# A transformer block on 16 images: LN2 without centring and with its scale transposed as a column, a fourth product in 96 jobs, ten bands of 30 convolved by TensorE, and a new order

## Chip, core and metric

The kernel runs on one core of a Trainium2 chip. The metric is device time of one launch in microseconds; the figure for the kernel before is the median of three runs.

## The reference

The input x is 16 images of 128 channels and 96 x 96 pixels in float32. With channels last, per image:

```python
xn1 = layernorm(x, ln1_w, ln1_b)              # over the 128 channels, for each pixel
q, k, v = xn1 @ wq.T, xn1 @ wk.T, xn1 @ wv.T  # 8 heads of 16 channels
q, k = l2norm(q), l2norm(k)                   # each channel over all 9216 pixels
attn = softmax(einsum('hcn,hdn->hcd', q, k) / 4)       # channels against channels
x = x + (attn @ v) @ wp.T
xn2 = layernorm(x, ln2_w, ln2_b)              # (x - mean) / sqrt(var + eps), then w and b
h1 = w_in @ xn2                               # 128 -> 512 channels
h2 = depthwise 3x3 convolution of h1, zero padding of one pixel
x = x + w_out @ gelu(h2)                      # 512 -> 128 channels
```

## The kernel before, in words

Channels lie on the 128 partitions, pixels along the free dimension. An image is 8 bands of 12 rows (1152 pixels), a band three units of 4 rows (384 pixels). The work of all 16 images is one stream: while the bands of an image go through the feed-forward part, the first norm of the next image is done beside them.

*Norms (`norm`).* Tiles of 512 pixels are brought to pixels-on-partitions by TensorE into one of four PSUM banks named h (`forth`). For LN1 (names with _a) this is a transpose of x (L662). For LN2 (_b) it is a product with the matrix `centre`, which subtracts the mean over channels as well (L658). ScalarE copies the tile to a buffer zT in SBUF (L694), VectorE takes its statistics with two bn_stats, of two 128-pixel groups each (L669, tile st), and GpSimd makes the variance (L674), raises it to the power -1/2 (L678, rstd) and multiplies zT by rstd (L700). For LN1 the scaled zT is also multiplied with itself into the Gram matrix (L707), from which `attention` makes one 128 x 128 matrix per image. TensorE then transposes zT back (`channels`, `back`, L745), and ScalarE places the result in the ring buffer xn of rows with a column of padding (L751; for LN2 with a bias, L749).

*Second x (`x2`).* TensorE applies the image's matrix to LN1's xn (`mix`, L610), ScalarE writes that into an x tile (L619), and GpSimd's DMA adds the input x onto it (L622).

*Feed-forward (`conv_job`, `by_matmuls`, `ffn_out`).* The 512 hidden channels are four chunks. A job is one chunk of one band. TensorE makes its hidden rows (L932) and ScalarE copies them into a padded buffer h1 (L937; two halo rows, L928). The nine taps of the convolution are divided by the centre tap, so that the centre costs no multiplication. Three of the eight others are products made by ScalarE (L948, tiles pr): one is added to h1 by GpSimd (L951, tile merged), one onto the other by an accumulating DMA (L973), and that sum onto the result by a second accumulating DMA (L976). VectorE does five as multiply-adds: the first reads h1 and merged (L960), the middle ones go on in the PSUM tile acc (L964), the last writes the result h3 (L960). ScalarE applies gelu (L980). In 41 bands the fourth chunk is no job: TensorE convolves it with nine matrices `comp` that combine input projection and tap (L1041), and gelu reads PSUM (L1051). Last, four products over the chunks (L1069), VectorE's addition onto x (L1076) and the store.

*The order.* Nothing in the stream is ordered by a loop. Each piece of work is registered with its engine, an estimate of its duration, a place (a turn plus a constant from the table `AT`, and a rank), and the buffers that it reads and writes. `Plan.order` then runs a list scheduler with buffer pools over all of them: an idle engine takes the ready piece of the lowest place, a result counts as there after its duration plus a margin (`SLACK`, `T_LAND` for DMAs). The order of starts becomes the program order of each engine, and the engines wait for one another by semaphores:

```python
def pe(ns, p, f, r, w):
    op("PE", ns, p, f, r, w, ns + 200 + SLACK, ns)
def dve(ns, p, f, r, w, two=False, own=120):
    op("DVE", ns, p, f, r, w, ns + 120 + SLACK, ns + own, two=two)
def add(p, f, r, w):
    op("POOL", 890, p, f, r, w, T_LAND + SLACK, dma=T_ADD)
```

An op marked `two` (a VectorE op with two SBUF operands, a GpSimd op on whole tiles) is kept by the plan from running beside another such op.

Of the kernel before, what the change touches and what calls it, by code (L numbers as in the profile page):

```python
# [9 lines left out]
F32 = mybir.dt.float32  # L10
# [13 lines left out]
TINY = 1e-20  # L24
# [8 lines left out]
FOURTHS = ()  # L33
# [3 lines left out]
QT = 4  # L37
# [7 lines left out]
PR_BUFS = 7  # L45
H3_BUFS = 8
ZT_BUFS = 7
IN_TURN = ("zT", "tr", "h3", "pr", "xb", "x1")
AT = dict(
    load_w=-15.9, weights=1106.95, zeros=-4389.1, load_a=-21.95, forth_a=-14.05, stats_a=1086.6,  # L50
    variance_a=-3642.25, power_a=-2095.25, pool_product=152.05, merge=-3089.75, scaled_a=-3192.7, gram=420.15,
    back_a=-250, place_a=-142.6, attention=-21.5, mix=810.75, residual=204, mixed=-263.1, add_x=-3629.7,
    forth_b=-10.3, stats_b=962.7, variance_b=-3011.35, power_b=-3726.4, shift_b=20.9, scaled_b=-4386.5,
    back_b=285.25, place_b=-290.45, halo=-471.5, hidden=418.3, kept=-390.75, products=-596.2, add_last=-2869,
    tap=3.65, add_first=-4251.35, gelu=-9.7, conv=421.7, conv_gelu=4.3, out=422.65, add=865.75, store=-21.95,
    mix_0=421.5, residual_0=864.15, mixed_0=-612, add_x_0=-4213.25, gram_0=419.75, forth_a_0=-276.85,
    forth_b_0=-13.8, stats_a_0=1145.4, stats_b_0=866.4, scaled_a_0=-4479.8, copied_a=-299.2, copied_b=-393.1,
    copied_a_0=-390.45, copied_b_0=-1293.75, scaled_b_0=-3010.5, back_a_0=420.4, back_b_0=262, place_a_0=-286.8,
    place_b_0=11.4, shift_b_0=22.8, late=384.05,
)  # L60
# [12 lines left out]
T_ADD, T_MOVE, T_LAND = 2950, 1400, 500  # L73
# [11 lines left out]
class Plan:  # L85
# [7 lines left out]
    def __init__(self, **pools):  # L93
        self.free = {p: list(range(n)) for p, n in pools.items()}
        self.slot = {}
        self.ops, self.writer, self.readers, self.users = [], {}, {}, {}
        self.dma = 0.0
        self.two = self.held = self.lost = 0.0
# [31 lines left out]
    def order(self):  # L130
# [38 lines left out]
        def dispatch(engine, time):  # L169
# [22 lines left out]
            elif engine == "POOL":  # L192
                rest = max(0, self.two - time)
                ns, result, own = rest + ns, rest + result, rest + own
                if o[9]:
                    self.held = time + ns
            if o[9] and engine == "DVE":
                rest = max(0, self.held - time)
                ns, result, own = rest + ns, rest + result, rest + own
# [44 lines left out]
def tile_restormer_block(  # L244
# [81 lines left out]
    per_unit = const.tile([P, NCH], F32, name="per_unit")  # L326
    nc.scalar.dma_start(out=dw, in_=w_dw.rearrange("(n p) o kh kw -> p n (o kh kw)", p=P))
# [17 lines left out]
    small = ctx.enter_context(tc.tile_pool(name="small", bufs=4))  # L345
# [43 lines left out]
    def x_unit(of, i, u):  # L389
# [5 lines left out]
        tr=TR_BANKS, bk=BK_BANKS, h=H_BANKS, g=1, batch=4, zT=ZT_BUFS, x1=X1_BUFS, xb=XB_BUFS, pr=PR_BUFS, h3=H3_BUFS  # L395
# [44 lines left out]

    def zeros(p):


        def around(t, r):
            nc.gpsimd.memset(t[:, : r * WP].rearrange("p (r w) -> p r w", w=WP)[:, :, :1], 0.0)
            nc.gpsimd.memset(t[:, r * WP :], 0.0)
# [3 lines left out]
        for t in h1s:  # L450
            op("POOL", 1000, at("zeros", p), lambda t=t: around(t, BR + 2), [], [("w", "in")], 1200)

    def weights(p):
# [66 lines left out]
        def shifts():  # L520

            nc.vector.tensor_tensor(none, w2, w2, ALU.mult)
            nc.vector.tensor_scalar(none, none, TINY * TINY, TINY, ALU.is_lt, ALU.mult)
            nc.vector.tensor_add(w2, w2, none)
# [629 lines left out]
```

## Time and profile before

| | us |
|---|---|
| median of three runs (lowest, highest) | 4097.78 (4095.37, 4105.1) |
| profiled execution, its own time | 4102.59 |
| its span | 4100.9 |
| TensorE (PE) busy | 3936.4 |
| VectorE (DVE) busy | 3904.0 |
| ScalarE (ACT) busy | 3718.0 |
| GpSimd (POOL) busy | 3456.0 |

The page comes from one execution. Busy time is the time in which an engine runs at least one instruction; a matmul in float32 shows as two passes (two instructions), a transpose as one. Matmul ends are modelled, so PE may show busy where it is not at its peak. PEld is TensorE's weight load. A row of the groups reads: line, engine, operation, output<-inputs, shapes, count | busy us, mean ns of one | idle us of the engine before them, and what ended it. A row of the waits reads: who <- for whom: us in total, times, longest.

### The profile page before, as it was taken

Reading aid. Unit: us, or ns where it says so; the run is one execution under the profiler, and the core shown is the slowest. Engines: PE = TensorE matmul, PEld = TensorE weight load, DVE = VectorE, ACT = ScalarE, POOL = GpSimd, SP = SyncE. Lnnn points to the kernel's source line nnn. Section 1 sums busy time; section 2 is a strip of 40 time slices with the busy share of each in tenths; the row PEclk is TensorE's granted clock in tenths of the full one; section 3 lists DMA queues with packets and bytes.
Section 4 is the critical chain, followed back from the end, with each engine's and each line's share of the span. In section 5 each row is a group of like instructions: output and inputs, shape, how many; then the busy total and the mean of one; then the engine's idle time right before and its main releaser. Section 6 shows DMA issues by size and latency. Waiting matters only on the chain.

```text
span 4100.9 us, 52028 instructions
## 1 busy us (share of the span) xinstructions
PE 3936.4 (96%) x17409; PEld 2593.9 (63%) x17409; DVE 3904.0 (95%) x4170; ACT 3718.0 (91%) x5675; POOL 3456.0 (84%) x3320
## 2 busy tenths in 40 slices
PE   8999999999999999999999999999999999999999
PEld 6666666666666666666666566666666666566555
DVE  6999999999999999999999999999999999999998
ACT  4999999999999989899999999989999999899985
POOL 5988888797898979889788888978989889788774
PEclk9999999999999999999999999999999999999999
DMA  2999999998999999999999999989999999988996
GB/s 84 192 190 198 192 194 191 191 211 180 205 194 200 199 186 211 185 194 197 187 203 193 196 190 201 212 183 200 193 200 213 188 202 192 199 185 180 198 182 139
DMA packets 192846, 782.20 MB, mean 191 GB/s; under 512 B 22337, under 2 KB 23745, under 8 KB 192577
## 3 DMA queue, kind: packets, MB, share of 16 engines
q0 software_dynamic: 153072, 627.05, 80.4%
q1 hardware_dynamic: 38256, 151.73, 10.4%
q8 instruction: 137, 2.24, 0.2%
q14 instruction: 133, 1.08, 0.1%
q10 hardware_dynamic: 1248, 0.09, 0.0%
HBM read 148.85 MB, written 75.50 MB: 55 GB/s over the span
## 4 chain that ended last, share of the span: by engine, by line
PE 31%; DVE 20%; DMA 11%; ACT 11%; POOL 9%; issue 5%; POOLq 0%; DVEq 0%; SPq 0%; ACTq 0%
PE h L1069 9%; DVE acc L964 9%; PE h L932 7%; DMA h<-pr 6%; PE h L1041 5%; ACT pr L948 4%; DVE acc L960 4%; DVE h L960 3%; POOL merged L951 3%; DMA x<-in_x_dram 3%; PE h L658 2%; PE h L610 2%; PE h L745 2%; DMA pr<-pr 2%; POOL zT L700 2%
## 5 line engine op out<-in xcount | busy, mean ns | idle before, releaser
L964 DVE SCALAR_TENSOR_TENSOR acc<-h,ratio,acc 128x1140 f32<-128x1140 f32 (+2 forms) x1416 | 1949.4, 1377 | 18.2
L948 ACT ACTIVATE pr<-h,ratio 128x1152 f32<-128x1152 f32 x1410 | 1782.5, 1289 | 45.2 <-DMA pr<-pr 27.3
L951 POOL TENSOR_TENSOR merged<-pr,h 128x1152 f32<-128x1152 f32 x470 | 1249.5, 2659 | 72.8 <-DVE acc L960 44.8
L1069 PE MATMUL h<-h,woutT 128*128 128x384 f32 x3072 | 1122.3, 489 | 11.7 <-DVE x L1076 7.1
L932 PE MATMUL h<-xn,winT 128*128 128x384 f32 (+2 forms) x2826 | 1086.4, 495 | 24.2 <-DVE x L1076 9.0
L1041 PE MATMUL h<-xn,comp 128*128 128x380 f32 (+2 forms) x2214 | 794.1, 483 | 2.8 <-ACT h L937 2.3
L1069 PEld LDWEIGHTS h<-h,woutT 128*128 128x128 f32 x3072 | 560.0, 191 | 350.1 <-issue 14.8
L960 DVE SCALAR_TENSOR_TENSOR acc<-h,ratio,merged 128x1152 f32<-128x1152 f32 x470 | 753.2, 1602 | 26.8 <-POOL merged L951 11.6
L932 PEld LDWEIGHTS h<-xn,winT 128*128 128x128 f32 x2826 | 506.3, 190 | 357.8 <-issue 36.6
L937 ACT COPY h<-h 128x384 f32<-128x384 f32 (+2 forms) x1413 | 670.8, 511 | 63.4 <-PE h L932 58.4
L976 POOL DMA_DIRECT2D h<-pr x470 | 496.0, 1056 | 253.3 <-PE h L1069 39.3
L960 DVE SCALAR_TENSOR_TENSOR h<-h,ratio,acc 128x1152 f32<-128x1152 f32 x471 | 662.0, 1406 | 7.6 <-PE h L1069 1.2
L980 ACT ACTIVATE h<-h 128x1152 f32<-128x1152 f32 (+1 forms) x473 | 561.4, 1187 | 101.7 <-DMA h<-pr 94.6
L973 POOL DMA_DIRECT2D pr<-pr x470 | 492.9, 1055 | 136.9 <-ACT pr L948 100.5
L1041 PEld LDWEIGHTS h<-xn,comp 128*128 128x128 f32 x2214 | 398.9, 190 | 229.3 <-ACT h L937 6.8
L745 PEld LDWEIGHTS h<-ident,zT 128*128 128x128 f32 x2232 | 273.5, 141 | 240.9 <-issue 81.3
L678 POOL TENSOR_TENSOR rstd_a<-ve_a,mhalf 128x4 f32<-128x4 f32 x288 | 416.4, 1521 | 1.0
L745 PE MATMUL h<-ident,zT 128*128 128x128 f32 x2232 | 357.5, 276 | 49.8 <-POOL zT L700 31.8
L700 POOL TENSOR_TENSOR zT<-zT,rstd_a 128x512 f32<-128x512 f32 x270 | 384.9, 1451 | 1.9
L678 POOL TENSOR_TENSOR rstd_b<-ve_b,mhalf 128x4 f32<-128x4 f32 x288 | 362.1, 1258 | 9.9
L700 POOL TENSOR_TENSOR zT<-zT,rstd_b 128x512 f32<-128x512 f32 (+1 forms) x288 | 357.7, 1243 | 5.2
L694 ACT COPY zT<-h 128x512 f32<-128x512 f32 x553 | 318.4, 613 | 38.2 <-PE h L658 28.0
(178 smaller groups left out, 4263.4 us busy)
## 6 DMA issues: line engine op xcount, KB each, us to landing
pr<-pr POOLq DMA_DIRECT2D x470, 576.0 KB, 7.0
h<-pr POOLq DMA_DIRECT2D x470, 576.0 KB, 7.3
x<-in_x_dram SPq DMA_DIRECT2D x128, 576.0 KB, 6.7
out_dram<-x SPq DMA_DIRECT2D x127, 576.0 KB, 5.4
x<-in_x_dram POOLq DMA_DIRECT2D x123, 576.0 KB, 7.5
out_dram<-x SPq DMA_DIRECT2D x3, 192.0 KB, 1.9
h<-in_L_conv_w_in_dram SPq DMA_DIRECT2D x1, 256.0 KB, 3.0
h<-in_L_conv_w_out_dram SPq DMA_DIRECT2D x1, 256.0 KB, 3.1
```

Source lines behind the costliest of these rows:

```text
L678: nc.gpsimd.tensor_tensor(rstd, d["ve"], mhalf, ALU.pow)
L700: engine.tensor_tensor(z, z, rstd.unsqueeze(2).to_broadcast([P, len(ks), P]), ALU.mult)
L745: nc.tensor.transpose(d["pB"][:, j * P : (j + 1) * P], zTs[q][:, k, :P], ident)
L932: nc.tensor.matmul(rows(ph), lhsT=winT[:, n, :], rhs=window(xn, r0 + r, e - r, 1), start=True, stop=True)
L937: nc.scalar.copy(window(h1_, r, e - r, 1), rows(d.pop(("ph", r))))
L948: nc.scalar.activation(to, shifted(t), AF.Copy, scale=ratio[:, n, t : t + 1])
L951: nc.gpsimd.tensor_tensor(merged, d["pr", dma_taps[0]], shifted(UNIT), ALU.add)
L960: nc.vector.scalar_tensor_tensor(to, shifted(t), ratio[:, n, t : t + 1], also, ALU.mult, ALU.add)
L964: nc.vector.scalar_tensor_tensor(to, shifted(t)[:, lo:hi, cut], ratio[:, n, t : t + 1], to, ALU.mult, ALU.add)
L980: nc.scalar.activation(h3, h3, AF.Gelu)
L1041: nc.tensor.matmul(d["pc"][:, lo:hi, cut], lhsT=comp[:, t, :], rhs=window(xn, r0 + dy, UR, dx)[:, lo:hi, cut], start=(t == order[0]), stop ...
L1069: nc.tensor.matmul(rows(d["po"]), lhsT=woutT[:, n, :], rhs=h3s[g, n][:, s * UR : (s + 1) * UR, :], start=(k == 0), stop=(k == NCH - 1),)
```

## The change

LN2's tiles are now plain transposes, they are not copied out of PSUM (the statistics read PSUM), and zT is not scaled or transposed back. Instead rstd, a column per 128 pixels, is broadcast along the free dimension and transposed by TensorE, which gives each channel's partition the scale of each pixel; VectorE multiplies x by it into xn. The centring is folded into the weights at the start (`centre` applied to `winT` and `comp`). LN2's bias is folded as well: h1's padding holds a constant in place of zero, each gelu adds a bias column `ksum` (another one for an image's first and last row, so there gelu is split), and the convolution by TensorE gets one more small product for the two edge columns (`edgeT`). As h1's padding now takes part, VectorE's taps run over the full width.

```diff
-PE_BANDS = (0, 3, 6, 10, 13, 16, 20, 23, 26)
+PE_BANDS = (0, 3, 6, 9, 12, 15, 18, 21, 24, 27)
-FOURTHS = ()
+FOURTHS = ((0, 1, (0,)),)
-PR_BUFS = 7
+PR_BUFS = 8
-ZT_BUFS = 7
+ZT_BUFS = 4
+BATCHES = 8
 AT = dict(
-    load_w=-15.9, weights=1106.95, zeros=-4389.1, load_a=-21.95, forth_a=-14.05, stats_a=1086.6,
+    load_w=-10696.6, weights=-1325.7, zeros=-1188.75, load_a=-32.75, forth_a=537.05, stats_a=22,
...
-RANK = dict(tap=-69.4, products=649.2, forth_a=-922.65, forth_b=-118.15, conv_gelu=-62.7, mix=-456.4)
+RANK = dict(tap=-712.55, products=1729.15, forth_a=-347.95, forth_b=-713.5, conv_gelu=-713.7, mix=-53.4)
+LATE = 400
-T_ADD, T_MOVE, T_LAND = 2950, 1400, 500
+T_ADD, T_MOVE = 2950, 1400
+T_LAND = 1000
...
             elif engine == "POOL":
-                rest = max(0, self.two - time)
+                rest = max(0, self.two - time) if k != self.ahead else 0
...
             if o[9] and engine == "DVE":
                 rest = max(0, self.held - time)
+                head = queues["POOL"][0][1] if queues["POOL"] and not idle["POOL"] else None
+                if head is not None and ops[head][9] and room(head) is None:
+                    rest, self.ahead = max(rest, self.pool_free + ops[head][1] - time), head
...
-    def inside(t, r0, n):
+    def inside(t, r0, n, padded=False):
-        cut = slice(max(0, 1 - dx), W - max(0, dx - 1))
+        cut = slice(0, W) if padded else slice(max(0, 1 - dx), W - max(0, dx - 1))
...
+        def centred_in():
+            pc = v["pc3"] = bank(("weights", "centred in"))
+            nc.tensor.matmul(pc, lhsT=centre, rhs=winT.rearrange("p n c -> p (n c)"), start=True, stop=True)
...
                 for k in range(QT):
-                    if second:
-                        nc.tensor.matmul(
-                            d["pT", q][:, k, :], lhsT=xt[:, j * P : (j + 1) * P], rhs=centre, start=True, stop=True
-                        )
-                    else:
-                        nc.tensor.transpose(d["pT", q][:, k, :], xt[:, j * P : (j + 1) * P], ident)
+                    nc.tensor.transpose(d["pT", q][:, k, :], xt[:, j * P : (j + 1) * P], ident)
...
-                nc.vector.bn_stats(d["st"][:, j, :], zT(qs[h])[:, k : k + 2, :P].rearrange("p t c -> p c t"))
+                of = d["pT", qs[h]] if second or DIRECT else zT(qs[h])[:, :, :P]
+                nc.vector.bn_stats(d["st"][:, j, :], of[:, k : k + 2, :].rearrange("p t c -> p c t"))
...
-            for h, q in enumerate(qs):
+            for h, q in enumerate(qs if not second else ()):
...
-                    nc.tensor.transpose(d["pB"][:, j * P : (j + 1) * P], zTs[q][:, k, :P], ident)
+                    if second:
+                        of = rstds[q // QB][:, q % QB * QT + k : q % QB * QT + k + 1].to_broadcast([P, P])
+                    else:
+                        of = zTs[q][:, k, :P]
+                    nc.tensor.transpose(d["pB"][:, j * P : (j + 1) * P], of, ident)
 
             def place():
                 if second:
-                    nc.scalar.activation(interior(i, u), rows(d["pB"]), AF.Identity, bias=b2)
+                    nc.vector.tensor_tensor(interior(i, u), rows(x_unit(xbs, i, u)), rows(d["pB"]), ALU.mult)
...
         def step(engine, ns, also=(), reads=(), writes=mine):
-                op(engine, ns, s, f, [("w", "qk"), *reads], [*writes, *also], ns + 200 + SLACK)
+                op(engine, ns, s, f, [("w", "qk"), *reads], [*writes, *also], ns + 200 + LATE)
...
         def gelu(s0, s1):
-            h3 = h3_of(g, n)[:, s0 * UR : s1 * UR, :]
-            nc.scalar.activation(h3, h3, AF.Gelu)
+            for r0, r1, z in row_parts(b, s0 * UR, s1 * UR):
+                h3 = h3_of(g, n)[:, r0:r1, :]
+                nc.scalar.activation(h3, h3, AF.Gelu, bias=ksum[:, z, n : n + 1])
...
+            if t == order[-1]:
+                for k0, k1, z in parts:
+                    nc.tensor.matmul(
+                        d["pc"][:, k0 - s * UR : k1 - s * UR, 0 : W : W - 1], lhsT=edgeT,
+                        rhs=ident[:6, 2 * z : 2 * z + 2].unsqueeze(1).to_broadcast([6, k1 - k0, 2]),
+                        start=False, stop=(k0, k1, z) == parts[-1],
+                    )
...
+    zeros(-17.0)
     weights(-17.0)
-    zeros(-17.0)
```

With `FOURTHS`, the jobs of the first chunk in an image's six inner bands (96 jobs) have four products; the fourth is added to merged by GpSimd in an op of its own (L1030 after; the code for it stood in the kernel before, unused).

What the new order does is seen on three engines at the same place of the program, LN2 of image 4. TensorE first: the three tiles of 512 pixels that hold the end of band 2 and most of band 3 (x2_4_2, x2_4_3) go into banks h_1 to h_3. Before:

```order
L658 MATMUL h_1_74<-centre_83,x2_4_2_7442 128x128 x3
L658 MATMUL h_1_74<-centre_83,x2_4_3_7550 128x128
L662 MATMUL h_2_75<-ident_78,x_5_4_7333 128x128 x4
L658 MATMUL h_3_76<-centre_83,x2_4_3_7550 128x128 x4
L1069 MATMUL h_0_73<-h3_2_151,woutT_119 128x384
L1069 MATMUL h_0_73<-h3_7_156,woutT_119 128x384
L745 MATMUL h_1_74<-ident_78,zT_4_161 128x128
L745 MATMUL h_1_74<-ident_78,zT_2_159 128x128 x2
```

After:

```order
L708 MATMUL h_1_74<-ident_78,x2_4_2_7383 128x128 x3
L708 MATMUL h_1_74<-ident_78,x2_4_3_7549 128x128
L708 MATMUL h_2_75<-ident_78,x2_4_3_7549 128x128 x4
L708 MATMUL h_3_76<-ident_78,x2_4_3_7549 128x128 x4
L1120 MATMUL h_0_73<-xn_128,comp_124 128x384
L1120 MATMUL h_0_73<-xn_128,comp_124 128x4x95
L1120 MATMUL h_0_73<-xn_128,comp_124 128x384
L1120 MATMUL h_0_73<-xn_128,comp_124 128x4x95 x2
L661 MATMUL h_1_74<-xn_128,mwT_4_7099 128x384
```

The three LN2 tiles now stand one behind the other in three of the four banks, the fourth bank takes a convolution by TensorE, and the mix (L661) is the next to use bank h_1. On VectorE the same tiles' statistics (st_b4_6 to st_b4_8) stood so before:

```order
L669 BN_STATS st_b4_6_7685<-zT_6_163 128x6
L960 SCALAR_TENSOR_TENSOR acc_77<-h1_0_137,ratio_106,merged_141 128x1152
L669 BN_STATS st_b4_6_7685<-zT_6_163 128x6
L964 SCALAR_TENSOR_TENSOR acc_77<-h1_0_137,ratio_106,acc_77 128x12x95
L1076 TENSOR_TENSOR x2_3_7_6750<-h_0_73,x2_3_7_6750 128x384
L964 SCALAR_TENSOR_TENSOR acc_77<-h1_0_137,ratio_106,acc_77 128x12x95
L669 BN_STATS st_b4_7_7729<-zT_1_158 128x6
```

and after, from between the first tile's two on:

```order
L1036 SCALAR_TENSOR_TENSOR acc_77<-h1_0_141,ratio_106,merged_145 128x1152
L716 BN_STATS st_b4_6_7717<-h_1_74 128x6
L1040 SCALAR_TENSOR_TENSOR acc_77<-h1_0_141,ratio_106,acc_77 128x1152
L716 BN_STATS st_b4_7_7735<-h_2_75 128x6
L1040 SCALAR_TENSOR_TENSOR acc_77<-h1_0_141,ratio_106,acc_77 128x1152
L716 BN_STATS st_b4_7_7735<-h_2_75 128x6
L1036 SCALAR_TENSOR_TENSOR h3_6_160<-h1_0_141,ratio_106,acc_77 128x1152
L716 BN_STATS st_b4_8_7758<-h_3_76 128x6
L1036 SCALAR_TENSOR_TENSOR acc_77<-h1_1_142,ratio_106,merged_145 128x1152
L716 BN_STATS st_b4_8_7758<-h_3_76 128x6
L1040 SCALAR_TENSOR_TENSOR acc_77<-h1_1_142,ratio_106,acc_77 128x1152
L812 TENSOR_TENSOR xn_128<-x2_4_2_7383,h_1_74 128x4x96
```

The statistics now read the banks themselves, each second one a tap behind the first, and the placing (L812, xn from x and a bank) has come to VectorE. On GpSimd the same tile's small ops before:

```order
L674 TENSOR_SCALAR ve_b4_6_7727<-st_b4_6_7685 128x4
L678 TENSOR_TENSOR rstd_a5_9_7731<-ve_a5_9_7631,mhalf_93 128x4
L678 TENSOR_TENSOR rstd_b4_6_7739<-ve_b4_6_7727,mhalf_93 128x4
L700 TENSOR_TENSOR zT_5_162<-zT_5_162,rstd_a5_9_7731 128x4x128
L700 TENSOR_TENSOR zT_6_163<-zT_6_163,rstd_b4_6_7739 128x4x128
```

and after:

```order
L1030 TENSOR_TENSOR merged_145<-merged_145,pr_5_151 128x1152
L725 TENSOR_TENSOR rstd_a5_11_7713<-ve_a5_11_7685,mhalf_93 128x4
L1049 DMA pr_7_153<-pr_4_150 128x1152
L1052 DMA h3_5_159<-pr_2_148 128x1152
L1049 DMA pr_1_147<-pr_0_146 128x1152
L1027 TENSOR_TENSOR merged_145<-pr_6_152,h1_1_142 128x1152
L751 TENSOR_TENSOR zT_2_164<-zT_2_164,rstd_a5_11_7713 128x4x128
L721 TENSOR_SCALAR ve_b4_6_7751<-st_b4_6_7717 128x4
L721 TENSOR_SCALAR ve_b4_7_7753<-st_b4_7_7735 128x4
L725 TENSOR_TENSOR rstd_b4_6_7755<-ve_b4_6_7751,mhalf_93 128x4
```

The scaling of zT for LN2 is gone; the whole-tile work that has come is the fourth product's addition (L1030).

On SyncE's queue the five weight loads stood behind the eight loads of image 0's x before and stand ahead of them now.

More of the change, by code (lines that the diff above doesn't have):

```diff
@@ L97, in __init__ @@
         self.dma = 0.0
-        self.two = self.held = self.lost = 0.0
+        self.two = self.held = self.lost = self.pool_free = 0.0
+        self.ahead = None
     def op(self, engine, ns, place, work, reads, writes, result, own=None, dma=0, two=False):
@@ L753, in place_row @@
             def place_row(r, row):
-                to = window(xn, r, 1, 1)
-                nc.scalar.activation(to, rows(d["pB"])[:, row : row + 1, :], AF.Identity, bias=b2)
+                nc.scalar.copy(window(xn, r, 1, 1), interior(i, u)[:, row : row + 1, :])
             copies = []
@@ L1024, in conv_job @@
             e = s + 1 if last else UPB
-            act(t_act((e - s) * UT), at("gelu", j), lambda s=s, e=e: gelu(s, e), [], h3[s:e])
+            ns = sum(t_act((y - x) * W, 1) for x, y, _ in row_parts(b, s * UR, e * UR))
+            act(ns, at("gelu", j), lambda s=s, e=e: gelu(s, e), [], h3[s:e])
     def by_matmuls(p, g, s):
```

144 lines of the change are left out of this document (106 added, 38 removed).

## The prediction

> **What bounds the kernel now.** I read the busy table first, then the windows, to see where the span is lost.
>
> ```profile
> PE 3936.4 (96%) x17409; PEld 2593.9 (63%) x17409; DVE 3904.0 (95%) x4170; ACT 3718.0 (91%) x5675; POOL 3456.0 (84%) x3320
> ```
>
> ```profile
> 0.00:50.00 50.00, 37.64 (x271) 34.44 (x272) 27.42 (x81) 19.50 (x39) 33.04 (x87) 1.00 0.38 123
> 50.00:100.00 50.00, 44.51 (x251) 33.32 (x250) 32.08 (x80) 23.77 (x48) 25.76 (x41) 0.93 0.17 45
> 100.00:4000.00 3900.00, 3757.32 (x16583) 2468.91 (x16582) 3763.03 (x3941) 3617.48 (x5511) 3356.08 (x3160) 0.99 0.93 195
> 4000.00:4050.00 50.00, 49.68 (x162) 29.25 (x161) 46.60 (x42) 41.42 (x56) 32.03 (x29) 1.00 0.83 172
> 4050.00:4101.00 51.00, 47.30 (x150) 27.98 (x148) 34.83 (x31) 15.84 (x24) 9.12 (x7) 0.99 0.45 104
> ```
>
> The columns are PE, weight load, VectorE (DVE), ScalarE (ACT) and GpSimd (POOL). Between 100 and 4000 us VectorE idles 3900 - 3763 = 137 us, and the first 100 us and the last 100 cost it 40 and 20 more. PE is as full, but its busy time hides slack: a group at its best runs eight passes in 2.59 us, 0.32 us each (first row below), where the group's average is 1122.3/3072 = 0.37 us. So VectorE sets the span, with PE close behind and the DMA engines (busy share 0.93) third. From the chain, the groups and the waits:
>
> ```profile
> 2592.00 2.59 PE h L1069 x8
> ```
>
> ```profile
> L964 DVE SCALAR_TENSOR_TENSOR acc<-h,ratio,acc 128x1140 f32<-128x1140 f32 (+2 forms) x1416 | 1949.4, 1377 | 18.2
> L948 ACT ACTIVATE pr<-h,ratio 128x1152 f32<-128x1152 f32 x1410 | 1782.5, 1289 | 45.2 <-DMA pr<-pr 27.3 <-POOL merged L951 13.2
> L951 POOL TENSOR_TENSOR merged<-pr,h 128x1152 f32<-128x1152 f32 x470 | 1249.5, 2659 | 72.8 <-DVE acc L960 44.8 <-ACT pr L948 20.6 <-ACT h L937 3.8
> L1069 PE MATMUL h<-h,woutT 128*128 128x384 f32 x3072 | 1122.3, 489 | 11.7 <-DVE x L1076 7.1 <-ACT h L937 3.2 <-ACT xn L755 1.1
> L932 PE MATMUL h<-xn,winT 128*128 128x384 f32 (+2 forms) x2826 | 1086.4, 495 | 24.2 <-DVE x L1076 9.0 <-ACT h L937 7.0 <-ACT zT L694 5.0
> L1041 PE MATMUL h<-xn,comp 128*128 128x380 f32 (+2 forms) x2214 | 794.1, 483 | 2.8 <-ACT h L937 2.3 <-DVE x L1076 0.4
> L960 DVE SCALAR_TENSOR_TENSOR acc<-h,ratio,merged 128x1152 f32<-128x1152 f32 x470 | 753.2, 1602 | 26.8 <-POOL merged L951 11.6 <-DVE h L960 0.9
> L980 ACT ACTIVATE h<-h 128x1152 f32<-128x1152 f32 (+1 forms) x473 | 561.4, 1187 | 101.7 <-DMA h<-pr 94.6 <-DVE h L960 5.7
> L700 POOL TENSOR_TENSOR zT<-zT,rstd_b 128x512 f32<-128x512 f32 (+1 forms) x288 | 357.7, 1243 | 5.2
> L694 ACT COPY zT<-h 128x512 f32<-128x512 f32 x553 | 318.4, 613 | 38.2 <-PE h L658 28.0 <-PE h L662 9.4
> L658 PE MATMUL h<-centre,x 128*128 128x128 f32 x2264 | 298.7, 277 | 21.7 <-DMA x<-in_x_dram 15.2 <-ACT h L937 3.3 <-ACT xn L751 1.7
> L669 DVE BATCH_NORM_STATS2 st_b<-zT 128x6 f32<-128x256 f32 x576 | 245.5, 428 | 21.5 <-ACT zT L694 21.1
> L749 ACT ACTIVATE xn<-h,b 128x384 f32<-128x384 f32 x384 | 225.9, 610 | 33.9 <-PE h L745 33.3
> L1076 DVE TENSOR_TENSOR x<-h,x 128x384 f32<-128x384 f32 x384 | 212.0, 552 | 66.8 <-PE h L1069 51.8 <-ACT xn L751 4.5 <-ACT h L937 2.1
> L662 PE MATMUL h<-ident,x 128*128 128x128 f32 x1080 | 159.4, 273 | 10.2 <-ACT zT L694 3.3 <-DMA x<-in_x_dram 2.4 <-ACT xn L749 1.4
> L846 PE MATMUL g<-ones,wide 128*128 128x1 f32 x60 | 10.9, 250 | 0.0
> ```
>
> ```profile
> PEld h L745 <- POOL zT L700: 67.1, 95, 4.3
> PE h L745 <- POOL zT L700: 31.8, 41, 4.1
> ```
>
> VectorE's largest single wait is the 51.8 us in which the last addition (L1076) waits for the fourth stage's product. PE's is on GpSimd's scaling of zT, 67.1 us at its weight loads and 31.8 us at the products.
>
> **The change, part by part.** VectorE first. Its ops overlap, so I price them by the step from start to start:
>
> ```profile
> 1019.39 0.43 DVE L669 BATCH_NORM_STATS2 st_b<-zT 128x6 f32<-128x256 f32 x1
> 1019.74 1.39 DVE L964 SCALAR_TENSOR_TENSOR acc<-h,ratio,acc 128x1140 f32<-128x1140 f32 x1
> 1021.04 0.43 DVE L669 BATCH_NORM_STATS2 st_a<-zT 128x6 f32<-128x256 f32 x1
> ...
> 1022.69 0.55 DVE L1076 TENSOR_TENSOR x<-h,x 128x384 f32<-128x384 f32 x1
> 1023.16 1.40 DVE L960 SCALAR_TENSOR_TENSOR h<-h,ratio,acc 128x1152 f32<-128x1152 f32 x1
> ...
> 1024.83 1.40 DVE L960 SCALAR_TENSOR_TENSOR acc<-h,ratio,merged 128x1152 f32<-128x1152 f32 x1
> 1026.26 1.41 DVE L964 SCALAR_TENSOR_TENSOR acc<-h,ratio,acc 128x1140 f32<-128x1140 f32 x1
> ```
>
> A tap with a small op behind it holds VectorE 1021.04 - 1019.74 = 1.30 us, one with the next tap of its sum behind it 1.43 us, a 128x384 op on PSUM and SBUF 0.47 us. *Taps.* Ten bands of 30 instead of nine make 45 bands by PE instead of 41, so four jobs of five taps go, and 96 jobs lose one tap to the fourth product: 116 fewer. In the order, 823 taps had a tap behind them and 1535 a small op; now it is 549 and 1693. That is -274 x 1.43 + 158 x 1.30 = -186 us. Full-width taps give back some 8 us:
>
> ```profile
> L964 DVE SCALAR_TENSOR_TENSOR acc<-h,ratio,acc 128x1140 f32<-128x1140 f32 x1062 | 1487.3, 1400 | 13.8
> L960 DVE SCALAR_TENSOR_TENSOR h<-h,ratio,acc 128x1152 f32<-128x1152 f32 x471 | 662.0, 1406 | 7.6 <-PE h L1069 1.2
> L964 DVE SCALAR_TENSOR_TENSOR acc<-h,ratio,acc 128x1045 f32<-128x1045 f32 x236 | 307.1, 1301 | 2.7
> L964 DVE SCALAR_TENSOR_TENSOR acc<-h,ratio,acc 128x1056 f32<-128x1056 f32 x118 | 155.0, 1313 | 1.7
> ```
>
> (957 at 6 ns, 234 at 12 ns.) *Placing.* 384 multiplications of x by the transposed scale move to VectorE, the same shape and memories as L1076: 384 x 0.47 = +180 us. *Setup* adds about 3 us net. VectorE's sum is -186 + 8 + 180 + 3 = **+5 us**. With mean durations (116 x 1.377 off, 384 x 0.552 on) it would be +52 us, the upper end; the lower, if no freed gap between taps were lost again, is -15 us.
>
> *Statistics.* 576 ops now read PSUM, elements 128 apart, instead of SBUF, 129 apart. No row shows that. L669's 428 ns for 256 elements lies near one element a nanosecond (1400 - 1301 = 99 ns for 95 columns), so a gain is excluded but for its fixed part; I take nothing, since L1076 with an operand in PSUM keeps that pace (552 ns for 384). [...]
>
> *The shared read.* A first tap (two SBUF operands) takes 1602 ns in the mean, 1422 in the median:
>
> ```profile
> L960 DVE SCALAR_TENSOR_TENSOR acc<-h,ratio,merged x470: 1396/1422/4212, 93.4 to 4064.5; 128x1152 f32<-128x1152 f32 x157
> ```
>
> 470 x 180 ns = 85 us are lost where GpSimd is in an op with two SBUF inputs. Of such GpSimd work (L951 and L700's LN2 rows, 1607 us) L700's 358 leave and the fourth products add 96 x 2.66 = 255 us: 85 x 103/1607 = -5 us. It could be -85 if the new order kept the two apart, or some +10.
>
> ScalarE: 84 more products (+108 us), 288 copies of zT gone (-177), 384 placements gone (-226), a bias column in every gelu (1289 - 1187 = 0.10 us each, 602 of them: +61), 128 more pieces at the image's edge (some +36), the four jobs (-8): about **-205 us**. GpSimd: -358 + 255 - 11 - 8 = **-122 us**. The DMAs lose eight of 1063 accumulations. PE: 1152 centring products in two passes become transposes in one, -2304 x 0.132 + 1152 x 0.148 = -134 us (rows L658 and L662); four bands more, 216 passes x 0.359 = +78; twelve hidden products less, 24 x 0.384 = -9; 146 edge products, 292 passes at the 0.18 of L846 = +53; setup +5: **-7 us**. None of these three is the bound, so their sums are worth nothing by themselves.
>
> *Start.* The five weight loads now go ahead of image 0's eight x loads on SyncE's queue, where a load holds the queue 8.03/7 = 1.15 us:
>
> ```profile
> 0.79 8.03 SPq L590 DMA_DIRECT2D x<-in_x_dram  x7
> ```
>
> In the first 50 us every engine waits for the one before it, so nothing covers that: 0 to 5 x 1.15 = 5.7 us, and as these loads are smaller I take **+4 us**.
>
> What is left is VectorE's idle time. (a) The statistics no longer wait for ScalarE's copy (21.1 us), but for the transposes: -10. (b) LN2's half of PE's 98.9 us on zT scaling goes, as the column needs only the power; a quarter of that 49 reaches VectorE: -12. (c) L1076's 51.8 us hang on gelus that wait 94.6 us for the accumulation into h3 (L980's row); the order now allows 1000 ns for a landing where it allowed 500, against a mean wait of about 1 us: half, -26. (d) Placing now waits for PE on VectorE; ScalarE lost 33.3 us so. In VectorE's queue a wait blocks taps behind it: +10. Together -38, with the port's -5: -43.
>
> Sum: 5 + 4 - 43 = -34 us against the profiled execution's own 4102.6 (4100.9 span and 1.7 around it), so 4068.6; that execution is 4.8 us above the median of 4097.8, so the forecast is **4064 us**.
>
> **Rivals.** *B, the idle stays.* The order's slips are not where I put them, and 5 - 5 + 4 leaves 4102 (4088 to 4116). For it: DMA at 0.93 is untouched. Against: three engines are lighter.
>
> *C, PSUM banks wait for VectorE (slower).* A tile of LN2 transposes was free after one ScalarE copy of 0.61 us. Now its bank stays until two statistics with taps between them are done, 0.35 + 1.30 + 0.35 us and about 0.7 for the tap under way: 2.1 us longer, for the 283 tiles in the four h banks 594 bank-us, or 150 us of a pool of four. Three such tiles stand in banks together in the PE order of image 4, with mix and hidden behind them. PE has 4101 - (3936 - 7) = 172 us unused; if half of the 150 lands on the path, 4098 + 5 + 4 + 75 = 4182 (4116 to 4218). It decides when PE's waits on VectorE pass what zT's scaling cost it.
>
> [...]
>
> *E, better than thought.* VectorE's steady idle of 137 halves, and the port's 85: 4098 - 111 + 9 = 3996 (3960 to 4042).
>
> *F, the change doesn't do what it says*: the column's transposes run as two-pass products; 1152 x 0.116 = +134 us takes PE to 4063 busy, and with half of its present 165 us of idle to about 4150.
>
> **How the numbers follow.** Forecast A 0.40 (4043 to 4086, the -43 at one and a half and at half), B 0.20, C 0.18, D 0.06, E 0.12, F 0.04. Within 0.3% of 4098 (12 us, about what a measurement of this kernel can tell from no change) lie 0.14 of B and 0.01 of A: 0.15. Faster: 0.39 of A, all E, 0.01 of B: 0.52. Slower: C, D, F and 0.05 of B: 0.33. The range 3990 to 4165 leaves out 0.05 of E, 0.08 of C, all D and 0.01 of F: 0.20.
>
> **What would show it.** VectorE busy near 3905 with the placing at about 550 ns and the statistics still at about 430; its idle near 155; ScalarE near 3510, GpSimd near 3330; PE's wait on zT halved; L1076's wait near 26. Wrong is the forecast if the busy sum moves by over 30 us, if statistics or placing cost more than their rows, or if PE waits on VectorE's reads of PSUM in place of GpSimd.

## The result and the profile after

The kernel after takes 4055.07 us (median of four runs, 4048.09 to 4061.62), the kernel before beside it 4097.53 (four runs): a ratio of 0.9893, 95% interval 0.9872 to 0.9914, or 42 us less. The forecast was 4064. The profiled executions took 4102.59 us before (span 4100.9) and 4061.62 after (span 4059.9); the granted clock was 0.994 and 0.996. The span lost 41.0 us.

The busy line of the page of the kernel after:

```profile
PE 3920.2 (97%) x16758; PEld 2516.4 (62%) x16758; DVE 3878.3 (96%) x4452; ACT 3579.4 (88%) x5204; POOL 3372.2 (83%) x3109
```

VectorE is busy 25.7 us less (3904.0 - 3878.3), and its idle time fell by 15.3 us, from 196.9 (4100.9 - 3904.0) to 181.6. These two make the 41.0. TensorE is 16 us less busy, and its idle time fell from 164.5 to 139.7 us.

The groups of the kernel after that answer to the rows of the prediction (busy us, mean ns | idle us before, and what ended it):

```profile
L1040 DVE SCALAR_TENSOR_TENSOR acc<-h,ratio,acc 128x1152 f32<-128x1152 f32 (+1 forms) x1308 | 1809.5, 1383 | 11.4
L1036 DVE SCALAR_TENSOR_TENSOR acc<-h,ratio,merged 128x1152 f32<-128x1152 f32 x466 | 692.6, 1486 | 28.3 <-POOL merged L1030 9.1 <-POOL merged L1027 7.0 <-DVE h L1036 0.5
L751 POOL TENSOR_TENSOR zT<-zT,rstd_a 128x512 f32<-128x512 f32 x270 | 333.5, 1238 | 8.7
L1030 POOL TENSOR_TENSOR merged<-merged,pr 128x1152 f32<-128x1152 f32 x96 | 259.1, 2699 | 3.8
L716 DVE BATCH_NORM_STATS2 st_b<-h 128x6 f32<-128x256 f32 x566 | 237.3, 422 | 9.6 <-PE h L708 8.9 <-ACT h L1013 0.4
L1168 DVE TENSOR_TENSOR x<-h,x 128x384 f32<-128x384 f32 x384 | 210.9, 549 | 39.7 <-PE h L1161 37.4 <-ACT xn L814 1.2 <-ACT pr L1024 0.6
L812 DVE TENSOR_TENSOR xn<-x,h 128x384 f32<-128x384 f32 x384 | 206.4, 547 | 25.3 <-PE h L808 20.5 <-ACT h L1013 1.1 <-ACT pr L1024 1.0
L808 PE MATMUL h<-ident,rstd_b 128*128 128x128 f32 x1152 | 188.0, 275 | 22.2 <-POOL rstd_b L725 14.9 <-DVE x L1168 2.4 <-ACT x L670 1.8
L1126 PE MATMUL h<-ident,edgeT 6*128 6x8 f32 (+2 forms) x292 | 54.2, 260 | 0.0
```

Placing (L812) costs VectorE 547 ns an op, the statistics of PSUM (L716) 422. The row that moved without being touched is the first tap's: 1602 ns in the mean before (L960), 1486 now (L1036). Four fewer of them at the usual 1.42 us are 5.7 of its 60.6 us; the other 55 us are the same op, with the same shapes, taking less time.

To see why, I took the timelines of VectorE and GpSimd over the whole span and sorted the first taps by whether a GpSimd op on a whole tile ran during them (an overlap of over 0.05 us). One such meeting in the kernel before, from its timeline (start us, us, engine, line):

```profile
1514.71 1.34 POOL L700 TENSOR_TENSOR zT<-zT,rstd_b 128x512 f32<-128x512 f32 x1
1514.95 2.34 DVE L960 SCALAR_TENSOR_TENSOR acc<-h,ratio,merged 128x1152 f32<-128x1152 f32 x1
...
1517.55 1.39 DVE L964 SCALAR_TENSOR_TENSOR acc<-h,ratio,acc 128x1140 f32<-128x1140 f32 x1
```

The scaling of zT began 0.24 us ahead of the tap and had 1.10 us to go; the tap took 0.92 us longer than its usual 1.42. Counted and added up:

| first taps | before | after |
|---|---|---|
| with no such GpSimd op beside them | 270, mean 1419 ns | 367, mean 1418 ns |
| beside the scaling for LN1 (zT, rstd_a) | 102, mean 1847 | 99, mean 1750 |
| beside the scaling for LN2 (zT, rstd_b), or both | 98, mean 1861 | none |
| beside a merge or a fourth addition | 0 | 0 |

The 98 taps beside LN2's scaling lost 98 x 0.44 = 43 us (six of them met LN1's as well; without these it is 0.37 us each), and that scaling is gone. Those beside LN1's lost 44 us before and 33 after. The merges and the fourth additions meet no first tap at all: they make the tile that the tap reads, and the next merge waits until the tap has read it (61.0 us in the waits below). GpSimd's small ops on variance and rstd cost a tap nothing that shows: 138 of the 270 taps in the first row of the table run beside one, and none of the 270 takes over 1.48 us.

The tap shown above began second and lost 0.92 of the 1.10 us that the scaling had left. So it went for most of the taps that met exactly one scaling in the kernel before: of the 72 that began behind it, 49 took over 1.5 us; of the 105 that began ahead of it, 89 took less. The other 16 began first and lost time all the same.

The waits of the kernel after (who <- for whom: us, times, longest):

```profile
ACT h L1057 <- DMA h<-pr: 61.3, 44, 5.5
POOL merged L1027 <- DVE acc L1036: 61.0, 114, 1.9
DVE x L1168 <- PE h L1161: 37.4, 46, 2.9
PEld h L808 <- POOL rstd_b L725: 25.8, 30, 2.8
DVE xn L812 <- PE h L808: 20.5, 27, 1.7
PE h L808 <- POOL rstd_b L725: 14.9, 14, 2.6
PEld h L1008 <- DVE xn L812: 9.7, 22, 1.0
PEld h L1008 <- DVE st_b L716: 7.5, 14, 1.4
PEld h L661 <- DVE st_b L716: 7.0, 15, 1.9
PEld h L808 <- POOL zT L751: 5.2, 6, 2.0
PE h L808 <- POOL zT L751: 3.5, 4, 1.8
```

TensorE's wait for GpSimd's scaling was 98.9 us before; its wait for LN2's rstd and LN1's scaling is 49.4 now (25.8 + 14.9 + 5.2 + 3.5). In place of what went come waits for VectorE: the three largest rows are shown, and all of TensorE's waits add up to 35 us for the statistics and 27 us for the placing. Its waits for the last addition fell meanwhile, from 68 to 35 us.

### The profile page after: what moved, and what is told of

It reads as the page before. It is cut to its first block, busy times and chain, and to the rows that moved or that the text cites. A ratio compares the mean times of both kernels' runs of the same rounds, so it can differ in the third digit from the quotient of the medians.

```text
span 4059.9 us, 50967 instructions
## 1 busy us (share of the span) xinstructions
PE 3920.2 (97%) x16758; PEld 2516.4 (62%) x16758; DVE 3878.3 (96%) x4452; ACT 3579.4 (88%) x5204; POOL 3372.2 (83%) x3109
## 5 line engine op out<-in xcount | busy, mean ns | idle before, releaser
L1040 DVE SCALAR_TENSOR_TENSOR acc<-h,ratio,acc 128x1152 f32<-128x1152 f32 (+1 forms) x1308 | 1809.5, 1383 | 11.4
L1120 PE MATMUL h<-xn,comp 128*128 128x380 f32 (+2 forms) x2430 | 892.1, 484 | 4.7 <-ACT h L1013 2.0
L1036 DVE SCALAR_TENSOR_TENSOR acc<-h,ratio,merged 128x1152 f32<-128x1152 f32 x466 | 692.6, 1486 | 28.3 <-POOL merged L1030 9.1
L1057 ACT ACTIVATE h<-h,ksum 128x1152 f32<-128x1152 f32 (+1 forms) x586 | 614.2, 1076 | 62.6 <-DMA h<-pr 61.3
L1036 DVE SCALAR_TENSOR_TENSOR h<-h,ratio,acc 128x1152 f32<-128x1152 f32 x467 | 654.9, 1402 | 11.1 <-PE h L1161 6.5
L708 PE MATMUL h<-ident,x 128*128 128x128 f32 x2212 | 322.7, 275 | 28.7 <-DMA x<-in_x_dram 9.6
L708 PEld LDWEIGHTS h<-ident,x 128*128 128x128 f32 x2212 | 262.5, 141 | 139.6 <-issue 48.6
L751 POOL TENSOR_TENSOR zT<-zT,rstd_a 128x512 f32<-128x512 f32 x270 | 333.5, 1238 | 8.7
L725 POOL TENSOR_TENSOR rstd_a<-ve_a,mhalf 128x4 f32<-128x4 f32 x288 | 309.1, 1074 | 16.9
L661 PE MATMUL h<-xn,mwT 128*128 128x384 f32 x768 | 289.8, 495 | 8.3 <-ACT x L670 2.5
L758 PEld LDWEIGHTS g<-zT 128*128 128x128 f32 x2160 | 271.0, 191 | 41.1 <-POOL zT L751 7.0
```

What stands on the lines that cost most here:

```text
L708: nc.tensor.transpose(d["pT", q][:, k, :], xt[:, j * P : (j + 1) * P], ident)
L725: nc.gpsimd.tensor_tensor(rstd, d["ve"], mhalf, ALU.pow)
L1036: nc.vector.scalar_tensor_tensor(to, shifted(t), ratio[:, n, t : t + 1], also, ALU.mult, ALU.add)
L1040: nc.vector.scalar_tensor_tensor(to, shifted(t)[:, lo:hi, cut], ratio[:, n, t : t + 1], to, ALU.mult, ALU.add)
L1057: nc.scalar.activation(h3, h3, AF.Gelu, bias=ksum[:, z, n : n + 1])
L1120: nc.tensor.matmul(d["pc"][:, lo:hi, cut], lhsT=comp[:, t, :], rhs=window(xn, r0 + dy, UR, dx)[:, lo:hi, cut], start=(t == order[0]), stop ...
```

## The experiments

Ratios are against the kernel before, run on the same chip; the kernel after stands at 0.9893. Four theories are told apart. L: LN2's scaling has left GpSimd, and first taps that met it are short again. P: the planner's new rule (a VectorE op of two SBUF operands waits for a whole-tile op that heads GpSimd's queue) makes them short. M: the doubled landing margin saves waits for the accumulating DMAs. D: what was gained is only a lucky order, which any other deal of the same work would lose.

**The planner's rule, taken out of the kernel after.**

```diff
-                head = queues["POOL"][0][1] if queues["POOL"] and not idle["POOL"] else None
-                if head is not None and ops[head][9] and room(head) is None:
-                    rest, self.ahead = max(rest, self.pool_free + ops[head][1] - time), head
```

> The kernel after, without the planner's new rule that lets a first tap wait for the GpSimd op at the head of its queue; every instruction stays, only the order is dealt anew. Theory P (the rule keeps first taps off GpSimd's two-operand ops, and that is where the 54 us of shorter first taps come from): the first tap's mean goes from 1486 back towards 1600 ns, VectorE's busy time up by about 50 us, time about 4100 us. Rival L (first taps are shorter because GpSimd lost the LN2 scaling and has less of such work): the mean stays at 1460 to 1510 ns and the time at 4045 to 4065 us.

Measured: 4068.77 us, 0.9904 (0.9889 to 0.9919). The first taps (groups):

```profile
L1033 DVE SCALAR_TENSOR_TENSOR acc<-h,ratio,merged 128x1152 f32<-128x1152 f32 x466 | 688.5, 1477 | 29.2 <-POOL merged L1027 12.1 <-POOL merged L1024 4.9 <-DVE h L1033 0.9
```

They are as short as with the rule, and the interval covers the ratio of the kernel after (the time itself lies 4 us above L's range, on a chip where the kernel before takes 4106 us). P falls here.

**The rule alone, put into the kernel before** (the same three lines, and the two places that read `ahead`).

> The kernel before, with only the planner's new rule added; same instructions, another order. Theory P: the first tap's mean falls from 1602 towards 1490 ns and the time by about 50 us, to 4050 us. Rival L: the mean stays within 1570 to 1630 ns and the time within 4085 to 4110 us.

Measured: 4170.9 us, 1.0156 (1.014 to 1.0171). Groups, then waits:

```profile
L966 DVE SCALAR_TENSOR_TENSOR acc<-h,ratio,merged 128x1152 f32<-128x1152 f32 x470 | 758.0, 1613 | 24.1 <-POOL merged L957 8.6 <-DVE h L966 0.5
```

```profile
DVE x L1082 <- PE h L1075: 108.9, 81, 5.5
```

First taps stay long (1613 ns in the mean), 201 of 470 beside a scaling. The loss is in the wait of the last addition for TensorE, 108.9 us where it was 51.8, and the time lies above the range of either theory. The rule deals the order anew, and does so worse than an unchosen deal of this kernel (1.0054, below), with no gain to set against it.

**The old places on the new work.**

```diff
-AT = dict(load_w=-10696.6, ...)   # RANK too
+AT = dict(load_w=-15.9, ...)      # both tables of the kernel before
```

> The kernel after with the table of places and ranks of the kernel before; same instructions. Theory O (the new table is what makes the new work fit): VectorE's busy time stays near 3880 us, its idle time rises by 50 us or more, time 4110 us or above. Rival W (the gain is in the work, any sensible table has it): time within 4045 to 4075 us.

Measured: 4126.89 us, 1.0044 (1.003 to 1.0059). Its busy line:

```profile
PE 3960.8 (96%) x16758; PEld 2534.5 (61%) x16758; DVE 3884.3 (94%) x4452; ACT 3583.3 (87%) x5204; POOL 3408.3 (82%) x3109
```

VectorE's busy time is that of the kernel after but for 6 us; its idle time is 247 us (span 4131.6) against 181.6. That is what O forecast. Seven orders of exactly the new work were run in all, most of them below, and VectorE is busy 3877 to 3891 us in them; in three orders of the old work it is busy 3893 to 3906 us. So the new work is cheaper for VectorE, but the order decides by how much, and how much of that the span gets.

**Without the fourth product.**

```diff
-FOURTHS = ((0, 1, (0,)),)
+FOURTHS = ()
```

> The kernel after without the fourth product: 96 taps more on VectorE, 96 products less on ScalarE, 96 additions less on GpSimd. If VectorE sets the span: 96 x (1.30 to 1.43) = 125 to 137 us more busy, less some 10 us of shared reads, time 4165 to 4190 us. Rival (PE and the DMAs bind as much, VectorE has slack): the time rises by less than 60 us.

Measured: 4152.96 us, 1.0106 (1.0089 to 1.0123). Page and groups:

```profile
PE 3959.0 (95%) x16758; PEld 2523.6 (61%) x16758; DVE 3995.0 (96%) x4548; ACT 3496.9 (84%) x5108; POOL 3107.8 (75%) x3013
```

```profile
L1036 DVE SCALAR_TENSOR_TENSOR acc<-h,ratio,merged 128x1152 f32<-128x1152 f32 x466 | 691.0, 1483 | 15.2 <-POOL merged L1027 1.6 <-DVE h L1036 0.5
```

VectorE is busy 117 us more for 96 taps, the span is 100 us longer; the time is 12 us below the range given for VectorE as the bound, and far above the rival's. GpSimd is 264 us lighter, and the first taps are no shorter for it: 1483 ns, against 1486. So the fourth additions don't hold them up.

**LN2's scaling put back on GpSimd, for nothing.** 288 multiplications of a scratch tile by rstd, 400 columns each where the old ones had 512.

```diff
+            if second:
+                scales = lambda: d["rstd"].unsqueeze(2).to_broadcast([P, QT, 100])
+                pool(QT * T_SCALED + 100, at("scaled" + ab, s, i), lambda: nc.gpsimd.tensor_tensor(
+                    idle, idle, scales(), ALU.mult), [bt], [("idle", 0)], True)
```

> The kernel after, and for each LN2 tile one more GpSimd multiplication of a 128 x 400 scratch tile by that tile's scale; nothing reads the scratch, so it adds only the two-operand GpSimd op that the change took away (400 columns instead of 512), and the output is untouched. Theory C (first taps got shorter because these 288 ops no longer meet them): the first tap's mean goes from 1486 to 1560 to 1610 ns, VectorE's busy time up by 35 to 55 us, and the time by 0.8 to 1.5% of the kernel before. Rival S (the shorter first taps come from the new order or the shorter queues): the mean stays below 1510 ns and the time within 0.4%.

Measured: 4143.32 us, 1.0103 (1.0086 to 1.012). Groups:

```profile
L1041 DVE SCALAR_TENSOR_TENSOR acc<-h,ratio,merged 128x1152 f32<-128x1152 f32 x466 | 717.5, 1540 | 31.9 <-POOL merged L1035 15.3 <-POOL merged L1032 4.1
L785 POOL TENSOR_TENSOR idle<-idle,rstd_b 128x400 f32<-128x400 f32 x288 | 337.0, 1170 | 2.7
```

and a meeting in its timeline:

```profile
1851.57 1.14 POOL L785 TENSOR_TENSOR idle<-idle,rstd_b 128x400 f32<-128x400 f32 x1
1851.73 2.21 DVE L1041 SCALAR_TENSOR_TENSOR acc<-h,ratio,merged 128x1152 f32<-128x1152 f32 x1
```

By the same count as above, 84 first taps now run beside an idle multiplication; the 81 that meet nothing else take 1620 ns. The mean of all goes from 1486 to 1540, about half of the way back to 1602, and VectorE's busy time rises by 32 us. The mean lies between the ranges of the two theories, the busy time just under C's and the time, 2.1% longer, above it. So L is shown in kind, and for half of its size. The idle ops are smaller, and each of these 81 meetings cost 0.20 us where one with LN2's scaling alone cost 0.37; why it is not more, no run here separates. Idle time rose as well, by 51 us; a new deal alone makes 10 to 15 us of that (next), the rest is unexplained.

**A new deal of the same work.** The DMA's planned time in the list scheduler is changed by 10 ns; no instruction is added or dropped, but the order of starts comes out differently.

```diff
-T_ADD, T_MOVE = 2950, 1400
+T_ADD, T_MOVE = 2960, 1400
```

> The kernel after with one estimate of the planner changed by 0.3% (an accumulating DMA at 2960 instead of 2950 ns): the same work with another order, neither better nor worse by any reason. Theory O (the table is fitted to one deal of the order): the time rises by 0.7 to 1.6% of the kernel before, to 0.997 to 1.005 of it, with VectorE's busy time the same. Rival W (the deal hardly matters, what counts is the work): within 0.4% of the kernel after, 0.985 to 0.993 of the kernel before.

Measured: 4079.8 us, 0.9952 (0.9938 to 0.9967), between the two ranges. A second deal, with 2940:

> A second neutral deal of the kernel after: the estimate of an accumulating DMA at 2940 instead of 2950 ns. Theory O (the kernel after stands at a chosen deal; others are worse by about as much as the first neutral deal): 0.3 to 1.0% above the kernel after, 0.992 to 0.999 of the kernel before, VectorE's busy time 3875 to 3890 us. Rival: deals scatter to both sides, and this one may as well be faster, 0.984 to 0.992.

Measured: 4079.73 us, 0.9935 (0.9911 to 0.9958); VectorE busy 3880.6. And the kernel before dealt anew, with 2960:

> A neutral deal of the kernel before: the same estimate at 2960 instead of 2950 ns. If the kernel before stands at a chosen deal as well, it is 0.5 to 1.6% slower, all in idle time, and the work of the change is worth what lies between neutral deals of both kernels, about 1.0 to 1.5%. If its deal is an ordinary one: within 0.3%, and the work by itself is worth only some 0.5%. The first tap's mean stays at 1590 to 1620 ns in both.

Measured: 4128.28 us, 1.0054 (1.0036 to 1.0073). Its busy line and its first taps:

```profile
PE 3939.7 (96%) x17409; PEld 2596.2 (63%) x17409; DVE 3893.3 (95%) x4170; ACT 3718.6 (90%) x5675; POOL 3462.2 (84%) x3320
```

```profile
L960 DVE SCALAR_TENSOR_TENSOR acc<-h,ratio,merged 128x1152 f32<-128x1152 f32 x470 | 738.5, 1571 | 37.9 <-POOL merged L951 24.8
```

The busy line and two waits of the first of the three:

```profile
PE 3929.0 (96%) x16758; PEld 2519.9 (62%) x16758; DVE 3883.3 (95%) x4452; ACT 3578.8 (88%) x5204; POOL 3390.6 (83%) x3109
```

```profile
DVE x L1168 <- PE h L1161: 49.0, 46, 5.7
DVE xn L812 <- PE h L808: 31.5, 36, 3.7
```

In this first one VectorE's busy time moved by 5 us, its idle time by 15 (4080.2 - 3883.3 = 196.9), its two waits for TensorE alone by 23 (they were 37.4 and 20.5). So these deals cost 0.4 to 0.6% of the kernel after and 0.5% of the kernel before, as if both tables of places had been chosen for their own work; the order without the planner's rule, above, is one more deal of the kernel after and costs 0.1%. D is wrong as an explanation of the whole gain: new deal against new deal, the new work stands at 0.9952 and 0.9935 where the old stands at 1.0054, 1.0 to 1.2% apart, as the chosen deals do (1.1%). But there is one such deal of the old work, and an edit that moves the time by less than some 0.6% can't be told here from its deal.

The gain is also made up otherwise between the new deals. The kernel before's first taps took 1571 ns in its new deal, outside the forecast of 1590 to 1620, and VectorE was busy 10.7 us less than in its chosen order, idle 29.5 us more (226.4). So the first taps of the two works differ by 79 to 100 ns between new deals (1571 to 1492 and 1471), which is 37 to 47 us where the chosen orders gave 55. VectorE's busy time differs by 10 to 13 us in place of 26, and 29 to 34 us lie in idle time.

**Nine bands instead of ten.**

```diff
-PE_BANDS = (0, 3, 6, 9, 12, 15, 18, 21, 24, 27)
+PE_BANDS = (0, 3, 6, 10, 13, 16, 20, 23, 26)
```

> The kernel after with nine bands of 30 convolved by TensorE as before: four jobs of five taps more on VectorE (20 x 1.3 to 1.4 = 27 us), 108 convolution products and 16 edge products less on PE (about 85 us). If VectorE is the bound alone: slower by 20 to 30 us. If PE binds as much as VectorE: the same within 10 us, or faster.

Measured: 4128.42 us, 1.0071 (1.0056 to 1.0086); VectorE busy 3922.0. Both forecasts missed: the four jobs that come back cost VectorE 44 us where 27 were expected, the time is 73 us longer than that of the kernel after and 49 longer than that of its first new deal. The ten bands are worth the 44 us of taps; the rest is about what a deal does.

**A second fourth product.**

```diff
-FOURTHS = ((0, 1, (0,)),)
+FOURTHS = ((0, 1, (0,)), (1, 1, (0,)))
```

> The kernel after with the fourth product in a second chunk too, 192 jobs: VectorE 96 taps less (about -125 us), ScalarE +122 us, GpSimd +255 us. If VectorE alone were the bound: down by 60 us or more, near 0.975 of the kernel before. If PE (3920 us busy) and the DMA engines stand right behind: within 25 us of the kernel after, since VectorE's gain turns into idle time.

Measured: 4180.1 us, 1.0194 (1.0179 to 1.0209). Page and waits:

```profile
PE 3970.0 (95%) x16758; PEld 2534.4 (61%) x16758; DVE 3797.9 (91%) x4356; ACT 3672.8 (88%) x5300; POOL 3680.7 (88%) x3205
```

```profile
DVE acc L1036 <- POOL merged L1030: 118.6, 85, 6.1
DVE x L1168 <- PE h L1161: 71.7, 72, 3.9
```

Neither forecast came out: the time is 125 us longer than that of the kernel after. VectorE gains 80 us of busy time and waits 118.6 us for GpSimd's additions where it waited 9.1. With 96 fourth products GpSimd is early enough; with 192 it is the engine that comes late, at 88% busy. Being that busy is not enough by itself: with the idle multiplications GpSimd was at 88% as well, and first taps waited 19 us for it. Whether a table of places chosen for 192 additions would take the wait away, no run shows.

**The old landing margin.**

```diff
-T_LAND = 1000
+T_LAND = 500
```

> The kernel after with the margin for a DMA's landing back at 500 ns. Theory M (the wider margin is what shortens the waits for the accumulation into h3 and, behind them, the last addition's wait for the fourth stage): ScalarE's wait on that DMA goes from 61 to 85 us or more, the last addition's wait on PE from 37 to 50 us or more, beyond the 49 us that a mere new deal of the order showed; time 0.8 to 1.5% above the kernel after. Rival D (any new deal of the order costs that much): ScalarE's wait stays at 55 to 70 us, time 0.3 to 0.8% above the kernel after.

Measured: 4104.24 us, 0.9997 (0.9983 to 1.0012). Waits:

```profile
ACT h L1057 <- DMA h<-pr: 81.8, 73, 4.0
DVE x L1168 <- PE h L1161: 49.8, 46, 3.7
```

It is slower than both new deals (0.9952, 0.9935), by 0.5 and 0.6%. ScalarE's wait for the accumulating DMA rises from 61.3 us to 81.8, between the ranges of M and D. With the wide margin it was 62.0 and 66.5 in the two deals, 72.8 with the weight loads moved (below), and 99.1 with the old table, so the margin's part in the rise is not shown. The last addition's 49.8 says nothing: it is 49.0 in a deal with the wide margin. M stays open, and with it a part of the gain: with the margin of the kernel before, the new work stands only 0.6% under the new deal of the old work (0.9997 against 1.0054), and VectorE's busy times there are 3891.4 and 3893.3 us. The kernel before with the wide margin was not run.

**The weight loads behind x again.**

```diff
-    load_w=-10696.6, ...
+    load_w=-15.9, ...
```

> The kernel after with the weight loads behind the eight x loads of image 0 on SyncE's queue, where they stood before. If the loads ahead cost time at the start: the first statistics start at 8 instead of 11 us, and VectorE's idle time before its first tap falls from 42 to 36 to 39 us. If later waits hide it: the first statistics start earlier, the idle time before the first tap stays at 40 to 44 us.

One run: 4073.11 us. The stretch up to the first tap, in windows of the kernel before, of the kernel after and of this one (PE, weight load, VectorE, ScalarE, GpSimd busy, clock, DMA share, GB/s):

```profile
0.00:93.40 93.40, 75.55 (x484) 63.03 (x485) 53.81 (x152) 36.67 (x76) 52.20 (x122) 0.96 0.27 85
```

```profile
0.00:107.10 107.10, 89.60 (x608) 73.53 (x609) 65.49 (x197) 38.75 (x80) 70.32 (x141) 0.97 0.26 86
```

```profile
0.00:115.30 115.30, 95.70 (x608) 77.96 (x609) 68.72 (x198) 38.86 (x80) 69.75 (x141) 0.97 0.25 80
```

VectorE idles 39.6, 41.6 and 46.6 us there. The first statistics start at 8.0 us with the loads behind x and at 11.3 with them ahead, but the first tap comes 8 us later. The 46.6 us are above both branches of the forecast. So the 4 us that I gave the loads ahead don't show; whether the loads gain any, one run within a deal's reach can't say.

No version here beats the kernel after.

## Why the prediction came out

The direction, the range and, within 9 us, the number were right. The terms were not: VectorE's busy time fell by 26 us where they made it zero, and its idle time by 15 where they said 34 (the 38, less 4 at the start). Two errors, of 26 and 19 us, cancelled, so that the number came so close is luck.

**The shared read, -5, is the step that failed.** It measured -55 (first taps), inside its bounds of -85 to +10. The loss of 85 us was read rightly from mean against median, but I spread it over all GpSimd work with two SBUF inputs. A shared read and a port, the prediction's names for this loss, are a mechanism that no run shows; the runs show that first taps beside a scaling took longer (1847 and 1861 ns in the mean, against 1419 with no whole-tile op beside them). The merges and the fourth additions can't meet a first tap, as its own input depends on them (none did, in either kernel). Of GpSimd's whole-tile ops only the scaling can (200 taps before, 99 after). The groups of the kernel before have LN1's beside LN2's row of 357.7 us:

```profile
L700 POOL TENSOR_TENSOR zT<-zT,rstd_a 128x512 f32<-128x512 f32 x270 | 384.9, 1451 | 1.9
```

LN2's part is 357.7/(357.7 + 384.9) = 48%, and 85 x 0.48 = 41 us was to be had from rows of the trace before. The taps counted in the timelines give 43 for LN2 and 11 more for LN1's meetings, which are a little fewer and cost less each (0.33 for 0.43 us). Part of the 55 belongs to the order: between new deals it is 37 to 47.

**VectorE's busy sum without that, +5, measured +29** (all but first taps 3150.8 to 3185.7, +34.9, of which 5.7 pay for the four first taps that are in my sum). The durations held, 547 ns for the placing where 552 was taken, 422 for the statistics where 428 was. To see what slipped, I counted each op in both timelines from its start to the next op's start, or to its own end where that comes first. The placing took 179.6 us, as priced (180), and the statistics changed by 0.9 us. The taps that went, with the wider ones, gave 159 us without the shared read, where my sum had 178: a tap's price was taken from one stretch. The small ops of set-up and attention took 12 us more where I had 3. (By this count the first taps gave 59 us in place of 55, and the rest comes to +33 in place of +29.)

**Idle time.** (a) Statistics: 21.1 to 8.9, -12 for -10; but LN1's statistics, which I left out, now wait 13.0 us for ScalarE's copy where they waited 1.9, and that takes most of it back. (b) TensorE's wait for the scaling: 98.9 to 49.4, halved as forecast, but LN2's part did not go: 41 us wait for its rstd, 9 for LN1's scaling, and 60 us of waits for VectorE have come. (c) The last addition: 51.8 to 37.4, -14 for -26; and 49.0 and 39.8 in the two new deals, so it is the order that sets it more than the margin. (d) Placing: +20.5 for +10. Start: +2 for +4.

**The other engines.** ScalarE -139 for -205, GpSimd -84 for -122, TensorE -16 for -7; as said there, none is the bound, and a wrong sum cost nothing. The fourth additions were 259 us for 255, the edge products 54 for 53.

**Rivals** (letters of the prediction). C came in part. The 35 us in which TensorE waits for the statistics are waits for banks, as no product reads st_b; of the 27 us for the placing, 16 are those of products that read xn, and may be for the data. Together they stayed under the 98.9 us that was its point of decision, and TensorE's idle time fell. (All of TensorE's waits for VectorE were 96 us before and are 118 now.) A kernel that copies LN2's tiles out of PSUM by ScalarE, which might take the waits for the statistics away, was not run. D (0.06 in the chances), by which the statistics would cost more from PSUM, is shown by no run: they took 422 ns with elements 128 apart in PSUM, 428 with 129 apart in SBUF. F is out: 1152 transposes of a broadcast column are 1152 instructions of 275 ns, where zT's took 276. B's reason, that the order decides where slips are, is borne out by the new deals: they move 10 to 30 us of VectorE's idle time, and the largest idle term of mine was 26.

## What to carry to other kernels

Where the mean of an op lies well above its median, list what ran beside the slow ones before pricing a change: work that the op depends on can't be among them, and the excess may hang on one or two other ops, of which one is about to leave. Where a planner sets the order, run the same work in two or three new deals first; their spread (0.1 to 0.6% here, most of it idle time) is the least effect that an edit can be credited with. A unit of work moved off the bound engine paid here (one fourth product, 1.5 to 2%) until the engine that took it came late (a second one, 2.4 to 3% slower than the first alone, in an order that was not chosen for it).

## What the runs showed of the hardware

A first tap that meets no scaling by GpSimd takes 1.40 to 1.48 us. One that meets a scaling loses 0.44 us in the mean in the kernel before and 0.33 in the kernel after; of the 200 before, 113 took under 1.5 us (median of these 1.42 us), and the slowest lost 2.8 us.

LN1's scaling, the same instruction in both kernels, took 1451 ns in the mean before and 1238 after. Its meetings with first taps are not the reason: the scalings that met no first tap became shorter by as much (1346 to 1150 ns) as those that met one (1576 to 1383). The cause stays open.

VectorE's statistics read elements that stand 128 apart in PSUM in 422 ns, and elements 129 apart in SBUF in 428. A column of 128 values, broadcast along the free dimension, is transposed by TensorE at the price of an ordinary tile (275 ns an instruction; 276 for zT before).
